# Seven products instead of eight in the first block of a gated layer's second projection, with its sums placed earlier and on two engines

## The chip, the cores and the metric

The kernel runs on one core of a Trainium2 chip. The metric is the time of one execution on the device, in microseconds (us); each figure of "the time" is a median of several runs. A profile is one further execution, taken by the hardware profiler; its engines are TensorE (PE, with its weight loads as PEld), VectorE (DVE), ScalarE (ACT), GpSimd (POOL) and SyncE (SP, which issues transfers here).

## The reference

A transformer block in float32 on x of shape (2, 1024, 256): self-attention (16 heads of 64), cross-attention to a context of shape (2, 154, 192), and a gated feed-forward layer, each with a layer norm before it and the input added after it. The part that matters here is the last:

```python
h = _layernorm(x, ln3_g, ln3_b)
p = h @ ff_w1 + ff_b1                    # (2048 tokens) x 256 x 2048
a, gate = (p[..., :D_FF], p[..., D_FF:]) # D_FF = 1024
h = a * gelu(gate) @ ff_w2 + ff_b2       # 1024 x 256
return h + x
```

## The kernel before

The first stages (self-attention, cross-attention) take the first 896 us, and nothing in them is touched. The order of instructions on each engine is the order in which the program writes them; nothing reorders it.

The gated layer takes the 2048 tokens in four **blocks** (`pair` 0 to 3) of 512 tokens, each seen as two halves j of 256. A block's first projection runs in `NF` = 8 steps (f), so there are 32 steps n. Each step has two half steps k = 2n and 2n + 1 in one loop (L1465 on): `gate_first(n)` and `gate_second(n)`. Step n's last product (`gate_last(n)`) is written inside `gate_first(n + 1)`.

The first projection is done with seven products instead of eight on a 2 x 2 partition (Strassen's method in Winograd's form): sums of weights (`weight_sums`) and sums of tokens (`token_sums`, four GpSimd instructions L1057 to L1060 a block) are made first. A step has seven 128x256 products on TensorE (L1074). VectorE takes them out of PSUM (L1103, L1105 in the first half step, L1119, L1122 in the second, L1131 in `gate_last`), ScalarE copies and makes the two gelus (L1099, L1117, L1123), and GpSimd multiplies value by gate into the layer's hidden tile `ub` (L1124 for half j = 1, L1133 for j = 0).

The second projection of a block starts when the block's hidden tile is complete, eight steps later, and is written into the half steps of the next block: the list `sums` is drained at two units a half step. It has two forms:

- `sum_slot`, the plain form, for block 0: 32 products of 128x256 (L1249), two a half step, k = 16 to 31, and four adds to x on VectorE (L1259).
- `fast_sum`, for the blocks in `FAST` (1 to 3): seven sums g of four 128x128 products each (L1219) per half j, one sum a half step, the first at k = 32. Sums 0 and 1 read hidden values as they are, sum 2 and later ones read weight sums (`quick_weights`, four 128x512 instructions L1181 to L1184) and token sums (`quick_tokens`, four 128x128 instructions a chunk c of two steps, L1196 to L1199, for each half j). Sum 0 of a half also brings an add to x on GpSimd (L1228), the others one each on VectorE (L1233).

`hold_quick` makes the tile in which the sums lie; its buffer was that of the cross-attention's transposed probabilities, last read at k = 5. `combos` is the list of sums still to be written; two a half step are taken from it. Before the change the weight sums are put there at k = 18, and block 1's token sums from k = 20 on.

Beside this, the norm of the second half of the tokens (batch entry 1) runs from k = 7 in steps at odd k, by the list `side`: a step's statistics (`stats`, two tiles, L242 and L243 on VectorE) go to the list `slow`, which `run_work` empties; one step later come the deviations (`deviation`, L248 and L252 on GpSimd), another step later the offset (L258 on VectorE) and two normalizations (L273 on GpSimd), and a step after that the transposes on TensorE (`turn`, L286). `later` holds bias adds on GpSimd (L326), one at each odd k from 17 on.

## Time and profile before

| | us |
|---|---|
| median of 3 runs | 1069.95 |
| lowest, highest | 1069.39, 1070.63 |
| the profiled execution | 1071.75 |
| its span, first to last instruction | 1069.1 |
| first product of the gated layer | 896.7 |
| block 0's second projection, first and last product | 942.0, 978.9 |
| first product of block 1's second projection | 980.8 |

A row of a timeline gives start (us from the span's start), duration, engine, line, operation, output<-inputs, shape, count, and in brackets the engine's idle time before it and what ended it. A row of the chain gives start, duration and what was done. A row of windows gives from:to, length, and for each engine its busy time and number of instructions. One fp32 matrix product is two TensorE instructions.

### The profile page before, as it was taken

The numbers are of one execution on the slowest core, as the hardware profiler recorded it, in microseconds if no ns is written. First come the engines' busy times: TensorE is split into PE (matmuls) and PEld (weight loads), VectorE is DVE, ScalarE is ACT, GpSimd is POOL, SyncE is SP. The second block draws the span as 40 slices with busy tenths as digits, with TensorE's granted clock in tenths as the row PEclk, the third lists the DMA queues.
The fourth block names the chain that finished last, engine by engine and source line by source line (L and its number), as shares of the span: only waits on it lengthen the run. The fifth ranks groups of instructions, "written<-read, shape, count | busy, mean of one in ns | idle before, by whom it ended". The sixth has DMA issues, their size and how long they took to land.

```text
span 1069.1 us, 48669 instructions
## 1 busy us (share of the span) xinstructions
PE 1057.3 (99%) x20228; PEld 709.8 (66%) x20228; DVE 882.9 (83%) x1321; ACT 645.3 (60%) x2096; POOL 774.8 (72%) x1652
## 2 busy tenths in 40 slices
PE   8999999999999999999999999999999999999998
PEld 6556756655555556657655655576866667788998
DVE  5789999998989989999999899978877887654554
ACT  5766667677666666666777676665666554342221
POOL 2677777778777777777777777676767876499984
PEclk9999999999999999999999999999999999999999
DMA  4132122021021121111102101126776545000000
GB/s 102 38 73 54 29 68 53 25 63 41 22 52 33 34 51 33 40 34 34 45 14 54 44 14 38 33 56 145 173 177 176 123 98 119 11 11 11 21 10 30
DMA packets 86046, 60.95 MB, mean 57 GB/s; under 512 B 32123, under 2 KB 74563, under 8 KB 85827
## 3 DMA queue, kind: packets, MB, share of 16 engines
q1 hardware_dynamic: 84450, 57.07, 22.0%
q8 instruction: 159, 2.61, 1.0%
q10 hardware_dynamic: 1376, 0.79, 0.2%
q14 instruction: 61, 0.49, 0.2%
HBM read 27.91 MB, written 2.10 MB: 28 GB/s over the span
## 4 chain that ended last, share of the span: by engine, by line
PE 92%; DVE 2%; DMA 2%; POOL 2%; SPq 1%; ACT 1%; issue 1%; DVEq 0%; POOLq 0%
PE po L578 20%; PE s L526 20%; PE py_ca L500 5%; PE py_sa L500 5%; PE pk_sa L369 5%; PE pq_sa L369 5%; PE pq_ca L369 5%; PE pv_sa L405 4%; PE poc L953 4%; PE pb L1074 4%; PE pq L1219 4%; PE sc L873 3%; PE pa L1074 2%; PE pc L1074 2%; PE pf L1249 1%; PE ph_ln L286 1%
## 5 line engine op out<-in xcount | busy, mean ns | idle before, releaser
L650 POOL TENSOR_SCALAR p<-p,rd,ee 128x512 f32<-128x512 f32 x512 | 390.4, 768 | 90.4 <-DVE rd L640 89.4
L537 ACT ACTIVATE p<-s,st 128x512 f32<-128x512 f32 x512 | 345.0, 686 | 175.6 <-DVE st L712 172.4
L712 DVE TENSOR_REDUCE st<-s 128x2 f32<-128x1024 f32 x256 | 308.9, 1207 | 59.6 <-issue 20.3
L675 DVE STREAM_TRANSPOSE pT<-p 128x1024 f32<-128x1024 f32 x256 | 302.8, 1220 | 2.1 <-POOL p L650 1.9
L526 PE MATMUL s<-k_sa,q_sa 64*32 64x512 f32 x4096 | 260.3, 591 | 0.8 <-DVE k_sa L390 0.6
L578 PE MATMUL po<-pT,held_v 64*32 64x256 f32 x8192 | 241.9, 376 | 0.4 <-DMA held_v<-held_v 0.4
L578 PEld LDWEIGHTS po<-pT,held_v 64*32 64x32 f32 x8192 | 177.3, 106 | 72.5 <-issue 25.2
L526 PEld LDWEIGHTS s<-k_sa,q_sa 64*32 64x32 f32 x4096 | 90.4, 106 | 91.6 <-issue 48.1
L890 ACT ACTIVATE p<-sc,neg 128x154 f32<-128x154 f32 x256 | 96.1, 404 | 76.1 <-DVE rden L898 73.3
L901 POOL TENSOR_SCALAR p<-p,rden 128x154 f32<-128x154 f32 x256 | 96.8, 399 | 49.2 <-DVE rden L898 49.0
L537 ACT ACTIVATION_READ_ACCUMULATOR p<-s,st 128x1 f32 x512 | 104.1, 203 | 0.0
L555 POOL TENSOR_TENSOR dd<-st 128x8 f32<-128x8 f32 x128 | 25.5, 199 | 71.9 <-DMA st<-st 68.5
L500 PE MATMUL py_ca<-ca_wo,o_ca 128*128 128x256 f32 x256 | 60.2, 383 | 0.0
L369 PE MATMUL pq_ca<-hT_ln,ca_wq 64*64 64x512 f32 (+1 forms) x576 | 59.4, 589 | 0.5 <-DMA ca_wq<-in_L_xattn_ca_wq_dram 0.5
L500 PE MATMUL py_sa<-sa_wo,o_sa 128*128 128x256 f32 x256 | 59.5, 386 | 0.0
L500 PEld LDWEIGHTS py_sa<-sa_wo,o_sa 128*128 128x128 f32 x256 | 47.3, 190 | 18.0 <-issue 5.0
L369 PE MATMUL pk_sa<-hT_ln,sa_wk 64*32 64x512 f32 x960 | 57.6, 590 | 0.4 <-ACT q_sa L384 0.4
L369 PE MATMUL pq_sa<-hT_ln,sa_wq 64*32 64x512 f32 (+1 forms) x976 | 57.7, 586 | 0.0
L879 DVE TENSOR_REDUCE neg<-sc 128x6 f32<-128x924 f32 (+1 forms) x48 | 47.8, 996 | 12.0 <-PE sc L873 11.8
L890 ACT ACTIVATION_READ_ACCUMULATOR p<-sc,neg 128x1 f32 x256 | 56.5, 221 | 0.0
L405 PE MATMUL pv_sa<-sa_wv,hT_ln 64*32 64x256 f32 x1792 | 53.7, 376 | 0.0
L917 DVE STREAM_TRANSPOSE pT_ca<-p 128x480 f32<-128x480 f32 (+1 forms) x96 | 52.9, 587 | 0.8 <-POOL p L901 0.8
(158 smaller groups left out, 1479.0 us busy)
## 6 DMA issues: line engine op xcount, KB each, us to landing
wf<-pT_ca SPq DMA_DIRECT2D x128, 128.0 KB, 2.4
st<-st SPq DMA_DIRECT2D x512, 1.0 KB, 1.8
held_v<-held_v SPq DMA_DIRECT2D x32, 256.0 KB, 4.1
sa_wq<-in_L_xattn_sa_wq_dram SPq DMA_DIRECT2D x32, 128.0 KB, 2.9
sa_wk<-in_L_xattn_sa_wk_dram SPq DMA_DIRECT2D x32, 128.0 KB, 3.2
sa_wv<-in_L_xattn_sa_wv_dram SPq DMA_DIRECT2D x16, 256.0 KB, 4.5
ca_wq<-in_L_xattn_ca_wq_dram SPq DMA_DIRECT2D x32, 128.0 KB, 3.8
wf<-in_L_xattn_ff_w_dram SPq DMA_DIRECT2D x12, 256.0 KB, 3.4
```

What stands on the lines that cost most here:

```text
L369: nc.tensor.matmul(pq[r][f:f + m, at:at + n], lhsT=wt[own, c, f:f + m], rhs=h[own, c, t0:t0 + n], start=(c == 0), stop=(c == NH - 1), tile ...
L405: nc.tensor.matmul(pv[r][f:f + KB, e * VC:(e + 1) * VC], lhsT=h[half, c, t0:t0 + KB], rhs=wt[half, c, :], start=(c == 0), stop=(c == NH - ...
L500: nc.tensor.matmul(py[:, e * D:(e + 1) * D], lhsT=o[:, i, (t + e) * P:(t + e + 1) * P], rhs=wo[kind][:, g * HP + i, :], start=(i == 0), st ...
L526: nc.tensor.matmul(sc[a4 * KB:(a4 + 1) * KB, j, :], lhsT=q[r, c:c + KB], rhs=k[r, h * HB:(h + 1) * HB], start=True, stop=True, tile_positi ...
L537: nc.scalar.activation(pr[:, j, :], sc[:, j, :], AF.Exp, bias=st[:, 0, 0, i, j:j + 1], accum_out=st[:, 0, 1, i, j:j + 1],)
L578: nc.tensor.matmul(po[a2][d:d + KB, :QH // 2], lhsT=v[e][r, t, d:d + KB], rhs=pT[r, d // DH * NK + n, :], start=(t == 0 and e == 0), stop= ...
L650: nc.gpsimd.tensor_scalar(pr[:, j, :], pr[:, j, :], own["rd"][:, c:c + 1], own["ee"][:, 0, c:c + 1], op0=ALU.mult, op1=ALU.mult,)
L675: nc.vector.transpose(halves[h][:, :, c:c + KB], slots[p]["p"][i].rearrange("p j (n k) -> p (j n) k", k=KB))
L712: nc.vector.tensor_reduce(st[:, 0, 0, i, :], sc[i], AX.X, ALU.max, negate=True)
L890: nc.scalar.activation(pr_[:, j, i, :T], sc[:, j, i * T:(i + 1) * T], AF.Exp, bias=neg[:, j, i:i + 1], accum_out=den[:, j, i:i + 1],)
L901: nc.gpsimd.tensor_scalar(pr_[:, j, i, :T], pr_[:, j, i, :T], rden[:, j, i:i + 1], 1.0, op0=ALU.mult, op1=ALU.mult,)
L1074: nc.tensor.matmul(into[:, :BT], lhsT=lhs, rhs=wh[pair][i], start=first, stop=True, skip_group_check=True)
```

## The change

- Block 0 takes the seven-product form too: `FAST` is now all four blocks.
- `hold_quick` and the weight sums move from k = 18 to k = 6; nothing is taken from `combos` before k = 6, and four a half step instead of two at k = 18 to 23.
- Block 0's token sums: half 0, chunks 0 and 1 go to GpSimd through `combos` (written at k = 8 to 11); half 0, chunks 2 and 3 go to VectorE through a list of their own, `in_turn`, two a half step (k = 12, 13, 16, 17); half 1, all four chunks, wait in the list `waiting` until k = 18 and then go to GpSimd (k = 18 to 21).
- In the gated layer `run_work` writes one tile's statistics a half step instead of all that stand in `slow`.

```diff
@@ run_work
-        if not spare["turned"]:
+        if slow and pools:
+            slow.pop(0)()
+        elif not spare["turned"]:
             flush(slow)
@@ gate_last
-        if pair in FAST and f % 2:
+        if pair == 0 and f % 2:
+            c = f // 2
+            (combos if c < 2 else in_turn).extend(
+                ((0, 0), fn) for fn in quick_tokens(0, 0, c, nc.gpsimd if c < 2 else nc.vector))
+            waiting.extend(((0, 1), fn) for fn in quick_tokens(0, 1, c))
+        elif pair in FAST and f % 2:
...
-    FAST = range(1, NPR)
+    FAST = range(NPR)
+    in_turn, waiting = [], []
@@ quick_tokens: the tile of the sums is looked up when a sum is written, not when it is listed
+        def s(i):
+            return quick["u", (2 * pair + j) % 4][:, (0, 1, None, 2)[i - 1], c, :]
...
-            lambda: tt(s1, a21, a22, ALU.add),
-            lambda: tt(s2, s1, a11, ALU.subtract),
+            lambda: tt(s(1), a21, a22, ALU.add),
+            lambda: tt(s(2), s(1), a11, ALU.subtract),
             lambda: tt(a21, a11, a21, ALU.subtract),
-            lambda: tt(s4, a12, s2, ALU.subtract),
+            lambda: tt(s(4), a12, s(2), ALU.subtract),
@@ the loop over half steps k
-            if k == 2 * NF + 2:
+            if k == 2 * len(CG):
                 hold_quick()
                 combos[:0] = [(None, fn) for fn in quick_weights()]
-            for _ in range(min(2, len(combos))):
+            elif k == 2 * NF + 2:
+                combos.extend(waiting)
+                waiting.clear()
+            n_mix = 0 if k < 2 * len(CG) else 4 if k in range(2 * NF + 2, 3 * NF) else 2
+            for _ in range(min(n_mix, len(combos))):
                 combos.pop(0)[1]()
+            for _ in range(min(2, len(in_turn))):
+                in_turn.pop(0)[1]()
```

(`NF` is 8 and `len(CG)` is 3, so `2 * len(CG)` is 6 and `2 * NF + 2` is 18.)

More of the change, by code (lines that the diff above doesn't have):

```diff
@@ L1187, in quick_tokens @@
     def quick_tokens(pair, j, c, engine=nc.gpsimd):
-        u, own = ub[pair][j], quick["u", (2 * pair + j) % 4]
+        u = ub[pair][j]
         (a11, a12), (a21, a22) = (
             [u[:, 2 * c + h, e * P:(e + 1) * P] for h in range(2)] for e in range(2))
-        s1, s2, s4 = (own[:, i, c, :] for i in range(3))
         tt = engine.tensor_tensor
         mixed[pair, j] = mixed.get((pair, j), 0) + 1
+        def s(i):
+            return quick["u", (2 * pair + j) % 4][:, (0, 1, None, 2)[i - 1], c, :]
         return [
-            lambda: tt(s1, a21, a22, ALU.add),
-            lambda: tt(s2, s1, a11, ALU.subtract),
+            lambda: tt(s(1), a21, a22, ALU.add),
+            lambda: tt(s(2), s(1), a11, ALU.subtract),
             lambda: tt(a21, a11, a21, ALU.subtract),
-            lambda: tt(s4, a12, s2, ALU.subtract),
+            lambda: tt(s(4), a12, s(2), ALU.subtract),
         ]
@@ L1206, in fast_sum @@
             [u[:, h::2, e * P:(e + 1) * P] for h in range(2)] for e in range(2))
-        assert g < 2 or mixed[pair, j] == NHF and (pair, j) not in [key for key, _ in combos]
+        assert g < 2 or mixed[pair, j] == NHF and (pair, j) not in [key for key, _ in combos + in_turn + waiting]
         lhs = (a11, a12, own[:, 1], a21, a22, own[:, 0], own[:, 2])[g]
```

## The prediction

> **What bounds the kernel now.** I read the page first, then the chain of waits, then engine busy time by window, then the timelines of GpSimd, VectorE and TensorE over the gated layer (894 us to the end).

> ```profile
> PE 1057.3 (99%) x20228; PEld 709.8 (66%) x20228; DVE 882.9 (83%) x1321; ACT 645.3 (60%) x2096; POOL 774.8 (72%) x1652
> ```

> TensorE is busy nearly always, so the end moves only if its work shrinks or it is made to wait. The chain gives the price of the work that is swapped:

> ```profile
> 942.14 0.86 PE pf L1249 x4
> 1053.48 12.52 PE pq L1219 x112
> ```

> A half step of the old form is two 128x256 products (four instructions), 0.86 us; block 0 has 64 such instructions, 16 x 0.86 = 13.8 us. The second row is the last block's second projection in seven products, 14 sums of 8 instructions with nothing between: 12.5 us. That is what block 0 will cost. TensorE saves 1.3 us.

> A half step k is one pass of the last loop: step n of the first projection is k = 2n and 2n+1. Block 0 is k = 0 to 15, its second projection starts at k = 16, block 1's at k = 32. The windows below run from the end of step 2's last GpSimd product (k = 6) to the end of step 15's (k = 32), and over the end of block 0.

> ```profile
> core 0: us, PE busy (x) PEld busy (x) DVE busy (x) ACT busy (x) POOL busy (x), PEclk, DMA share, GB/s
> 921.10:982.40 61.30, 60.22 (x288) 51.60 (x288) 35.46 (x92) 21.36 (x49) 52.29 (x88) 1.00 0.03 9
> 925.20:940.20 15.00, 13.92 (x65) 10.72 (x65) 12.56 (x37) 5.83 (x14) 12.55 (x22) 1.00 0.00 1
> ```

> Over these 61.3 us GpSimd works 52.3 and is free 9.0. In the second window VectorE and GpSimd both work 12.6 of 15.0 us, and this is the one place where TensorE loses time (1.1 us). The clock is 1.00. GpSimd is thus the second bound just where the change adds to it. Its rows:

> ```profile
> 920.40 0.73 POOL L1133 TENSOR_TENSOR held_v<-own 128x256 f32<-128x256 f32 x1 [5.58 <-DVE own L1131]
> 924.77 0.72 POOL L1124 TENSOR_TENSOR kT<-own 128x256 f32<-128x256 f32 x1 [3.64 <-ACT own L1123]
> 926.88 0.73 POOL L1133 TENSOR_TENSOR held_v<-own 128x256 f32<-128x256 f32 x1 [1.38 <-DVE own L1131]
> 927.56 0.72 POOL L1057 TENSOR_TENSOR hs<-hT_ln 128x256 f32<-128x256 f32 x1
> 930.42 0.72 POOL L1124 TENSOR_TENSOR kT<-own 128x256 f32<-128x256 f32 x1
> 932.17 0.73 POOL L1133 TENSOR_TENSOR held_v<-own 128x256 f32<-128x256 f32 x1
> 934.71 1.09 POOL L273 TENSOR_SCALAR xn_ln<-x,rstd_ln,off_ln 128x256 f32<-128x256 f32 x2
> 935.76 0.73 POOL L1133 TENSOR_TENSOR held_v<-own 128x256 f32<-128x256 f32 x1
> 940.56 0.72 POOL L1124 TENSOR_TENSOR kT<-own 128x256 f32<-128x256 f32 x1
> 947.84 0.73 POOL L1133 TENSOR_TENSOR u<-own 128x256 f32<-128x256 f32 x1
> 948.52 1.28 POOL L1181 TENSOR_TENSOR quick<-wf 128x512 f32<-128x512 f32 x1
> 951.10 0.73 POOL L1124 TENSOR_TENSOR u<-own 128x256 f32<-128x256 f32 x1
> 955.74 0.46 POOL L1196 TENSOR_TENSOR quick<-u 128x128 f32<-128x128 f32 x1
> 958.20 0.73 POOL L326 TENSOR_TENSOR x<-x,ff_b 128x256 f32<-128x256 f32 x1
> 979.50 0.73 POOL L1124 TENSOR_TENSOR u<-own 128x256 f32<-128x256 f32 x1 [0.64 <-ACT own L1123]
> 981.69 0.72 POOL L1133 TENSOR_TENSOR u<-own 128x256 f32<-128x256 f32 x1
> 982.38 1.00 POOL L1228 TENSOR_TENSOR x<-x,ends 128x384 f32<-128x384 f32 x1
> 983.34 0.46 POOL L1196 TENSOR_TENSOR quick<-u 128x128 f32<-128x128 f32 x1
> 1056.81 0.65 POOL L1197 TENSOR_TENSOR quick<-quick,u 128x128 f32<-128x128 f32 x1
> ```

> Prices, from start to start: a 128x256 product 0.7 (947.84 to 948.52); two weight sums 2.6 (948.52 to 951.10); the four token sums of one chunk 1.8 (955.74 to 958.20 is 2.46, less one product 0.7); the bias add of a half block 1.0 (982.38 to 983.34); block 1's four sums of the normed tokens 2.9 (927.56 to 930.42); one product with the norm's deviation pair 1.75 (930.42 to 932.17), so 1.05 for the pair; two normalizations 1.05 (934.71 to 935.76).

> ```profile
> 924.06 0.42 DVE L242 BATCH_NORM_STATS2 st_ln<-x 128x6 f32<-128x256 f32 x1
> 924.62 0.39 DVE L242 BATCH_NORM_STATS2 st_ln<-x 128x6 f32<-128x256 f32 x1
> 932.24 0.68 DVE L258 SCALAR_TENSOR_TENSOR off_ln<-mv_ln,rstd_ln 128x2 f32<-128x2 f32 x1
> 933.92 0.45 DVE L1131 SCALAR_TENSOR_TENSOR own<-pb,cols,own 128x256 f32<-128x256 f32 x1
> 934.28 0.42 DVE L1103 TENSOR_TENSOR own<-pb,own 128x256 f32<-128x256 f32 x1
> 939.08 0.48 DVE L1119 SCALAR_TENSOR_TENSOR own<-pb,cols,own 128x256 f32<-128x256 f32 x1 [0.46 <-PE pb L1074]
> 939.51 0.42 DVE L1122 TENSOR_TENSOR own<-pc,own 128x256 f32<-128x256 f32 x1
> 1054.48 0.53 DVE L1196 TENSOR_TENSOR quick<-u 128x128 f32<-128x128 f32 x1 [0.47 <-POOL u L1124]
> 1055.04 0.43 DVE L1197 TENSOR_TENSOR quick<-quick,u 128x128 f32<-128x128 f32 x1
> 1055.40 0.81 DVE L1198 TENSOR_TENSOR u<-u 128x128 f32<-128x128 f32 x1
> 1056.13 0.28 DVE L1199 TENSOR_TENSOR quick<-u,quick 128x128 f32<-128x128 f32 x1
> 1056.34 1.54 DVE L1228 TENSOR_TENSOR x<-x,ends 128x384 f32<-128x384 f32 x2
> ```
> ```profile
> 934.75 0.70 PE L1074 MATMUL pb<-hT_ln,wf 128*128 128x256 f32 x2 [0.74 <-DVE own L1103]
> 936.67 0.59 PE L1074 MATMUL pb<-hs,wf 128*128 128x256 f32 x2
> 983.03 1.05 PE L1219 MATMUL pq<-wf,u 128*128 128x128 f32 x8
> ```

> A chunk's statistics cost VectorE 0.56 (924.06 to 924.62), four token sums there 1.9 (1054.48 to 1056.34). The PE row at 934.75 is the old stall: two pairs of statistics and an offset stood ahead of L1103. The offset (L258) at 932.24 began as its deviation ended on GpSimd (932.17): no margin.

> **The change, part by part.**

> Seven products for block 0: minus 1.3 us of TensorE, as above. VectorE gets 12 adds for 4, after k = 16. Outside the second window it works 35.5 - 12.6 = 22.9 us of 46.3, half the time, so I cost that at nothing; if that cover were gone, it would be eight adds of at most 0.42 (L1122's row, twice their size), 3.4 us.

> Weight sums: 5.2 us of GpSimd, moved from k = 18 and 19 to k = 6 and 7. Their cover is the idle time before 924.77; the first two fit there (921.1 to 923.7), the last two, queued behind the product at 924.77, run 925.5 to 928.0 and push everything behind them, step 3's product first, 1.2 us late.

> Token sums: 32 instructions, 24 on GpSimd. Eight stand at k = 8 to 11 (3.6 us), sixteen at k = 18 to 21 (7.1). Two bias adds, at k = 16 and 23, bring 2.0. So GpSimd gets 12.7 us more between k = 6 and k = 32, the weight sums aside.

> Where that ends: block 1's second sum (983.03) reads the product that GpSimd started at 981.69 and ended at 982.4, a margin of 0.6. From here GpSimd's lateness is TensorE's. With all 9.0 us of idle filled, the excess is 12.7 - 9.0 - 0.6 = 3.1 us; 1.1 of the idle cannot be filled (923.7 to 924.8 comes before the product it waits for), so 4.2. What TensorE saved ahead of this point is contained in it.

> The waits add to that. GpSimd's queue after the change: step 3's product ends at 928.7, the four normed-token sums 931.6, two token sums 932.5, step 4's first product 933.2, two more 934.1, deviation about 935.0 (before: 932.2). VectorE stands at that offset from 932.2 to 935.0 with step 5's evacuations queued behind it: offset to 935.7 (0.68), one statistic 936.3, L1131 and L1103 (0.36, 0.42) 937.1, and only then the product that started at 934.75. TensorE is 2.4 us late.

> GpSimd goes on: product 935.7, two token sums 936.6, product and two sums 938.1, deviation 939.1, normalizations 940.2, step 5's last product 940.9 (before: 936.5). Here the new wait bites. VectorE's first two token sums, at k = 12, read that product, so VectorE stands until 940.9; then two sums (0.95), a statistic, and L1119 (0.43) to 942.8. Step 6's next TensorE product needs that L1119: 942.85 where it was 936.67, 6.2 late. And GpSimd waits in turn: L1122, the gelu and its product take 1.05 from L1122's start (939.51 to 940.56), so it idles from 940.9 to 943.8. Product, deviation, normalizations, product: 947.3. The same loop leaves it idle some 0.7 before step 7's first product and 1.3 before step 8's (estimates by the same steps; VectorE's sums at k = 16 again wait for step 7's last product). So 948.0 + 0.7 + 1.05 + 1.05 + 0.7 = 951.5, the bias add 952.5, idle to 953.8, and 0.7 + 1.05 + 0.7 + 0.7 (product, normalizations, a 0.7 bias row, product): what ended at 948.5 (947.84, k = 18) ends at 956.9.

> From there to step 15's product GpSimd took 33.8 us (948.6 to 982.4), 0.64 of it idle (979.50). It loses the weight sums (5.2) and gets 7.1 + 1.0: 33.8 - 0.6 - 5.2 + 8.1 = 36.1. So 956.9 + 36.1 = 993.0, and block 1's second sum starts there, not at 983.03: 10.0 later. TensorE, 6 to 7 us late by its own waits and 1.3 ahead by its sums, could be there by 989, so GpSimd sets it. Behind it GpSimd has 3.2 us a step (two products, four token sums) against TensorE's 4.8 (seven products of 0.43, two sums of 12.52/14), and all goes as before.

> Spread statistics: they take away most of the old stall (up to the window's 1.1 us), but the offsets' wait takes its place. Nothing is gained as long as GpSimd is late.

> [...]

> Sum: +10.0 us. The profiled execution took 1071.75 us (span 1069.1 and 2.65 around it); it would take 1081.75. The median of the runs is 1069.95, so 1080.0.

> **The rivals.**

> *Packing only, 1074.* The VectorE waits cost GpSimd no further idle time, and 4.2 us are left. For it: the 9.0 us of idle. Against: each wait is in a queue in order. Chance 0.21.

> *The cover holds, faster: 1067.5.* GpSimd's early sums vanish in its idle time before 927, the spread statistics end TensorE's 1.1 us of stall and the 1.3 come too: minus 2.4. It decides if GpSimd's excess at k = 33 stays under the 0.6 margin. Against: 12.7 us against 9.0. Chance 0.07.

> *Both by halves, within 0.2%.* The excess is some 2 us, as if a token sum were cheaper than its row. 0.2% of the time (2.1 us) is about what a measurement of this kernel tells from no change. Chance 0.06.

> *The engines hinder each other, 1083.* The GpSimd row at 1056.81 took 0.65 rather than 0.46 while VectorE added two operands (1056.34): 0.2 us for each overlap, and eight token sums and their loop make some 3 us. [...] Chance 0.10.

> **How the numbers follow.** The forecast has 0.56. Slower are 0.56 + 0.21 + 0.10 = 0.87, same 0.06, faster 0.07. The range goes from below the packing case, 1073, to above the last, 1084; about 0.17 is left out (0.13 below, the rest above).

> **What would show it.** Right: the first two weight sums before step 3's product, GpSimd near 9 tenths from 925 to 993, TensorE idle some 8 us between 930 and 953 behind VectorE's evacuations and 2 to 4 us near block 1's first sums behind GpSimd, VectorE's token sums waiting for the GpSimd product, seven-product sums at 0.89 a half step in block 0. Wrong: step 15's product ending before 984, or TensorE without idle time at k = 8 to 16.

## The result, and the profile after

| | before | after the change |
|---|---|---|
| median, us | 1069.95 (5 runs, 1068.08 to 1070.63) | 1079.58 (5 runs, 1078.89 to 1081.25) |
| the profiled execution | 1071.75 | 1081.25 |
| its span | 1069.1 | 1079.5 |
| start of step 2's last GpSimd product (k = 6) | 920.40 | 919.29 |
| from there to the end | 148.7 | 160.2 |

The change made the kernel slower: ratio 1.0096, interval 1.0085 to 1.0107. From k = 6 to the end it takes 11.5 us longer (160.2 - 148.7). What lies ahead of that is untouched by the new sums, and in the profiles below it ends anywhere between 919.3 and 922.2 us. So the stretch from there to the end, and not the span, is what I compare between profiles; it is called the gated part. In the changed kernel the numbers of the later lines are two to eleven higher (in its variants by a few more): L1103 is L1105, L1119 is L1121, L1131 is L1133, L1133 is L1135, the token sums are L1207 to L1210, the second projection's matmul is L1230.

The page of the changed kernel, busy times, granted clock by slice, and shares of the chain:

```profile
PE 1061.9 (98%) x20276; PEld 710.7 (66%) x20276; DVE 886.9 (82%) x1337; ACT 646.9 (60%) x2098; POOL 790.5 (73%) x1678
...
PEclk9999999999999999999999999999999999899999
...
PE 83%; POOL 7%; DMA 3%; DVE 2%; SPq 2%; ACT 1%; issue 1%; POOLq 0%; ACTq 0%; DVEq 0%
```

TensorE has less to do and is yet busy 4.6 us longer (1061.9 against 1057.3), and one slice shows a lower clock (8 tenths where the others have 9): some of its work ran slowly. GpSimd holds 7% of the chain, where it held 2%: the chain now runs through it from the weight sums at 924.38 to the product that ends at 993.5, with few breaks, the longest of them TensorE's from 941.53 to 946.85.

Busy time by window, the changed kernel (columns: PE, PEld, DVE, ACT, POOL, then the granted TensorE clock):

```profile
921.10:982.40 61.30, 55.87 (x298) 48.02 (x297) 35.50 (x98) 19.37 (x45) 52.34 (x92) 0.92 0.02 7
...
925.00:993.00 68.00, 60.67 (x321) 52.06 (x319) 37.37 (x104) 21.15 (x50) 59.91 (x109) 0.91 0.03 9
930.00:953.00 23.00, 17.91 (x74) 13.53 (x72) 11.34 (x34) 5.91 (x14) 17.17 (x32) 0.78 0.00 1
...
936.00:946.00 10.00, 8.39 (x21) 5.63 (x22) 4.80 (x17) 2.17 (x5) 7.13 (x14) 0.51 0.01 2
```

In the 61.3 us that the prediction counted, GpSimd is free 9.0 us, as before, though it has 12.7 us more to do: the work did not fill the gaps, it moved the end. Step 15's product comes 73.5 us behind the start of the gated part (992.82 less 919.29) where it came 61.3 behind it (981.69 less 920.40), 12.2 later. From 936 to 946 TensorE's granted clock is 0.51. Before, it was 1.00 in the whole stretch. There is a second, shorter fall of the clock near block 1's first sums, behind TensorE's wait there:

```profile
987.48:990.89 3.41, 1.52 (x10) 1.25 (x9) 0.20 (x1) 0.42 (x2) 3.33 (x8) 1.00 0.00 0
990.89:994.31 3.42, 3.19 (x13) 2.63 (x12) 0.91 (x2) 0.83 (x2) 3.42 (x6) 0.50 0.01 2
```

The waits of TensorE from 915 to 1000 (engine, line, whom it waited for: total, times, longest), and the timelines of the three engines, all of the changed kernel:

```profile
PE pb L1076 <- DVE own L1105: 3.4, 1, 3.4
PE pq L1230 <- POOL u L1135: 2.1, 2, 1.9
PE ph_ln L286 <- POOL xn_ln L273: 1.0, 1, 1.0
PE pb L1076 <- DVE own L1121: 0.9, 2, 0.5
```
```profile
923.66 0.73 POOL L1126 TENSOR_TENSOR kT<-own 128x256 f32<-128x256 f32 x1 [1.06 <-ACT own L1125]
...
933.20 0.71 POOL L252 TENSOR_TENSOR rstd_ln<-var_ln,power 128x2 f32<-128x2 f32 x1
...
939.17 0.73 POOL L1135 TENSOR_TENSOR held_v<-own 128x256 f32<-128x256 f32 x1
942.43 0.73 POOL L1126 TENSOR_TENSOR kT<-own 128x256 f32<-128x256 f32 x1 [2.53 <-ACT own L1125]
...
947.91 0.73 POOL L1126 TENSOR_TENSOR kT<-own 128x256 f32<-128x256 f32 x1 [1.94 <-ACT own L1125]
...
951.42 1.00 POOL L1239 TENSOR_TENSOR x<-x,ends 128x384 f32<-128x384 f32 x1
954.24 0.73 POOL L1126 TENSOR_TENSOR u<-own 128x256 f32<-128x256 f32 x1 [1.82 <-ACT own L1125]
...
956.70 0.73 POOL L1135 TENSOR_TENSOR u<-own 128x256 f32<-128x256 f32 x1
...
992.82 0.72 POOL L1135 TENSOR_TENSOR u<-own 128x256 f32<-128x256 f32 x1
```
```profile
933.95 0.67 DVE L258 SCALAR_TENSOR_TENSOR off_ln<-mv_ln,rstd_ln 128x2 f32<-128x2 f32 x1 [3.14 <-POOL rstd_ln L252]
...
939.94 0.29 DVE L1207 TENSOR_TENSOR quick<-held_v 128x128 f32<-128x128 f32 x1 [3.73 <-POOL held_v L1135]
940.26 0.29 DVE L1208 TENSOR_TENSOR quick<-quick,held_v 128x128 f32<-128x128 f32 x1
...
951.50 1.07 DVE L1207 TENSOR_TENSOR quick<-held_v 128x128 f32<-128x128 f32 x1 [2.04 <-POOL held_v L1135]
```
```profile
935.92 0.91 PE L1076 MATMUL pb<-hT_ln,wf 128*128 128x256 f32 x2 [3.42 <-DVE own L1105]
...
941.53 1.22 PE L1076 MATMUL pb<-hs,wf 128*128 128x256 f32 x2 [0.51 <-DVE own L1121]
942.55 1.06 PE L1076 MATMUL pb<-hs,w1s 128*128 128x256 f32 x2
943.40 1.06 PE L1076 MATMUL pc<-hs,w1s 128*128 128x256 f32 x2
...
993.60 0.79 PE L1230 MATMUL pq<-wf,u 128*128 128x128 f32 x2 [0.23 <-POOL u L1135]
```

They tell one story. VectorE stands 3.14 us at the offset, because GpSimd's deviation (933.20) is behind the weight sums and four token sums; L1105 is queued behind that, and TensorE waits 3.42 us for it. VectorE stands again, 3.73 us, at its first token sum until GpSimd's product of 939.17 is done; L1121 follows, TensorE goes on at 941.53, and now GpSimd has to wait for what TensorE starts so late: 2.53, 1.94 and 1.82 us. From 956.70 GpSimd is packed (it works nearly without a pause), and block 1's sum at 993.60 waits for its product. The products at 942.55 and 943.40 stand 0.85 us apart, where two of before stood 0.43 apart (941.12 and 941.55): that is the clock, 0.50 in those us where it was 1.00 before.

### The profile page after: what moved, and what is told of

It is laid out like the page before. It is cut to its first block, busy times and chain, and to the rows that moved or that the text cites. A ratio compares the mean times of both kernels' runs of the same rounds, so it can differ in the third digit from the quotient of the medians.

```text
span 1079.5 us, 48811 instructions
## 1 busy us (share of the span) xinstructions
PE 1061.9 (98%) x20276; PEld 710.7 (66%) x20276; DVE 886.9 (82%) x1337; ACT 646.9 (60%) x2098; POOL 790.5 (73%) x1678
## 4 chain that ended last, share of the span: by engine, by line
PE 83%; POOL 7%; DMA 3%; DVE 2%; SPq 2%; ACT 1%; issue 1%; POOLq 0%; ACTq 0%; DVEq 0%
PE po L578 18%; PE s L526 18%; PE py_ca L500 5%; PE py_sa L500 5%; PE pq_ca L369 4%; PE pq_sa L369 4%; PE pv_sa L405 4%; PE pk_sa L369 4%; PE poc L955 4%; PE pq L1230 3%; PE sc L875 3%; PE pb L1076 3%; DMA st<-st 2%; SPq L547 2%; PE pa L1076 2%; PE pc L1076 2%
## 5 line engine op out<-in xcount | busy, mean ns | idle before, releaser
L578 PEld LDWEIGHTS po<-pT,held_v 64*32 64x32 f32 x8192 | 177.0, 106 | 73.5 <-issue 27.6
L881 DVE TENSOR_REDUCE neg<-sc 128x6 f32<-128x924 f32 (+1 forms) x48 | 47.8, 997 | 12.6 <-PE sc L875 12.4
```

The costliest lines, as they stand in the source:

```text
L578: nc.tensor.matmul(po[a2][d:d + KB, :QH // 2], lhsT=v[e][r, t, d:d + KB], rhs=pT[r, d // DH * NK + n, :], start=(t == 0 and e == 0), stop= ...
```

## The experiments

The theory: the loss is GpSimd's queue ahead of block 1's first sums, made longer by VectorE standing in order behind it (offset, token sums). The first rival: the amount of the work alone, wherever it is done. The clock came in after the first profile. The kernel before was measured again with each group of runs; a ratio is to its median there, which was 1070.95 us for the first three runs below and for kept_warm.

**VectorE's eight token sums to GpSimd** (pool_tokens), which takes away the second wait and makes GpSimd's load larger:

```diff
-            (combos if c < 2 else in_turn).extend(
-                ((0, 0), fn) for fn in quick_tokens(0, 0, c, nc.gpsimd if c < 2 else nc.vector))
+            combos.extend(((0, 0), fn) for fn in quick_tokens(0, 0, c))
```

> The changed kernel, but half 0's chunks 2 and 3 are summed on GpSimd as well (eight sums, 3.6 us more work there) and none on VectorE. Theory (VectorE standing in its queue for GpSimd is what widens the loss): VectorE no longer stands for 3.7 us at k = 12 and 2.0 us at k = 16, so GpSimd does not idle 2.5 and 1.9 us before the products of steps 6 and 7; those 4.4 + 1.8 us go, 3.6 come. Step 15's last product is some 2.9 us earlier and the time falls to 1076.7 (1075 to 1078), though GpSimd does more. Rival (GpSimd's amount of work alone sets the time): 3.6 us slower, 1083.

Measured: 1079.49 us, ratio 1.0084 (1.0069 to 1.0099); gated part 157.7, so 2.5 less than the change (1.7 less than its repeat below) with eight more instructions on GpSimd. That is less than was forecast, and the interval overlaps the change's; the rival's 1083 is excluded. TensorE's waits and GpSimd's row ahead of step 7's first product:

```profile
PE pb L1076 <- DVE own L1105: 3.4, 1, 3.4
PE pq L1229 <- POOL u L1135: 2.4, 1, 2.4
...
```
```profile
946.98 0.73 POOL L1126 TENSOR_TENSOR kT<-own 128x256 f32<-128x256 f32 x1 [0.62 <-ACT own L1125]
```

The wait behind L1121 is gone and GpSimd's idle time there falls from 1.94 to 0.62. The amount of work alone would have made it slower. The offset's wait, 3.4, stays, as it should.

**Half 1's sixteen token sums left out** (half1_out); that half's products read plain tiles:

```diff
-            waiting.extend(((0, 1), fn) for fn in quick_tokens(0, 1, c))
...
+        if (pair, j) == (0, 1):
+            lhs = (a11, a12, a11, a21, a22, a12, a21)[g]
```

> The changed kernel, but the sixteen token sums of block 0's half 1 (k = 18 to 21) are left out, and its sums 2 to 6 read hidden values that were not summed. Theory (GpSimd's lateness at k = 33 is paid by TensorE a second time): GpSimd reaches step 15's product 7.1 us earlier, at about 986.4, before TensorE asks for it; the stalls at block 1's first two sums and the slow products behind them go, 4.1 us, 1075.5 (1074.5 to 1076.5). Rival (only the first stall, before 946 us, costs): no change, 1079.6.

Measured: 1077.84, ratio 1.0066 (1.0051 to 1.0081), above the forecast range, though the kernel before was itself 1.0 us slower here than in the result; gated part 155.4, 4.8 less (4.0 less than the repeat). TensorE's waits no longer name GpSimd's `u`:

```profile
PE pb L1076 <- DVE own L1105: 3.4, 1, 3.4
PE pb L1076 <- DVE own L1121: 0.9, 2, 0.5
PE ph_ln L286 <- POOL xn_ln L273: 0.7, 1, 0.7
```

So GpSimd's load from k = 18 on is on the path to the end, as its packing says, and 6.7 of the 11.5 us are there without it.

**All 32 left out** (no_tokens; the products of block 0 read plain tiles):

```diff
-            (combos if c < 2 else in_turn).extend(
-                ((0, 0), fn) for fn in quick_tokens(0, 0, c, nc.gpsimd if c < 2 else nc.vector))
-            waiting.extend(((0, 1), fn) for fn in quick_tokens(0, 1, c))
+            pass
...
+        if pair == 0:
+            lhs = (a11, a12, a11, a21, a22, a12, a21)[g]
```

> The changed kernel, but all 32 token sums of block 0 are left out, and its sums 2 to 6 read hidden values that were not summed; the early weight sums, the spread statistics, seven products and the two bias adds stay. Theory (the whole loss comes from where the token sums are done): what stays are 1.3 us saved and at most 1.2 us of GpSimd's weight sums running into k = 8: 1069.3 (1068.0 to 1070.5). Rival (the early weight sums or the spreading cost as much): 1072 or more.

Measured: 1069.64, ratio 0.9988 (0.9978 to 0.9998), as the theory had it; gated part 149.5, 0.8 above before. The token sums are thus 10.7 of the 11.5 us by the profiles and all of the loss by the ratios (0.9988 against 1.0096). The profiled execution is one of the slower ones: the mean granted clock was 1.000 in eight of the ten executions, which took 1067.9 to 1070.4 us, and 0.998 in the two that took 1071.9 and 1072.4, the profiled one among them. Without the token sums the seven products do save time, 0.2 to 2.4 us by the interval.

**The weight sums alone moved** (weights_early: before with the weight sums at k = 6):

```diff
-            if k == 2 * NF + 2:
+            if k == 2 * len(CG):
```

> The kernel before with one edit of the change: the weight sums at k = 6 and 7. Theory: their last 1.2 us push GpSimd's queue, VectorE stands for the offset at k = 11 that much longer ahead of two statistics, TensorE stalls some 2 us at k = 13 and may be granted half its clock for one stretch: 1.2 to 2.8 us slower, ratio 1.0011 to 1.0026. Rival (they vanish in GpSimd's idle time, which was the cover that the edit counts on): 1.0000.

Measured: 1072.85 against 1071.65, ratio 1.0008 (0.9999 to 1.0017), under the forecast range and not clear of no change; gated part 149.7, 1.0 more. The old stall grows from 0.74 to 1.77 us, the product's row being

```profile
937.55 0.70 PE L1074 MATMUL pb<-hT_ln,wf 128*128 128x256 f32 x2 [1.77 <-DVE own L1103]
```

**The statistics alone spread** (spread_alone: before with the edit in `run_work`):

```diff
-        if not spare["turned"]:
+        if slow and pools:
+            slow.pop(0)()
+        elif not spare["turned"]:
```

> The kernel before with one edit of the change: one tile's statistics a half step. Theory: the old stall at VectorE's statistics shrinks by some 0.5 us, but the transposes at k = 15 wait for GpSimd's normalizations, whose queue is as long as before, and take it back: 0 to 0.5 us faster, ratio 0.9995 to 1.0000 to the kernel before. Rival (the stall of 1.1 us was VectorE's alone): 1.1 us faster, 0.9990.

Measured: 1070.27 against 1071.65, ratio 0.9993 (0.9985 to 1.0002); the stall is 0.6 where it was 0.74. Nothing that can be told from no change.

**Full clock by extra work** (kept_warm: the change with 30 transposes of the identity put on TensorE ahead of the second half of step 6, for nothing but to keep it busy):

```diff
+            if k == 2 * NF - 3:
+                warm = sum_tile("warm")
+                for _ in range(30):
+                    nc.tensor.transpose(warm[:, :P], ident, ident)
```

> The changed kernel with 30 transposes of the identity put into TensorE's queue ahead of the second half of step 6 (k = 13), where TensorE stands 3.4 us; they fill the wait and nothing reads them. What is asked: between 936 and 946 us products follow each other at 0.85 us rather than 0.43, and the granted clock was 0.84 to 0.90 there. If TensorE's idle time brings the low clock, the products behind stay at 0.43, GpSimd gets its inputs sooner, and the time falls by 1 to 2 us, to 1078. If the clock comes from something else, no change or 0 to 1 us slower.

Measured: 1082.08, ratio 1.0105 (1.009 to 1.012): a miss. Windows:

```profile
937.00:941.00 4.00, 1.98 (x10) 1.06 (x9) 0.66 (x3) 0.47 (x1) 3.84 (x9) 1.00 0.00 0
943.00:948.00 5.00, 5.00 (x12) 4.01 (x13) 3.40 (x12) 2.16 (x5) 3.38 (x6) 0.50 0.00 0
```

The clock was kept at the first wait and fell after the next ones (1.66, 0.21 and 1.29 us, from 938 to 943). The time came out where the other branch of the expectation had it, but not for its reason. One place was not enough, so the clock's price was still open.

**Full clock at every wait** (all_warm: transposes at four places):

```diff
+        if n == NF - 1:
+            keep_warm(10)
...
+            if k == 2 * NF - 3:
+                keep_warm(30)
...
+            if k == 2 * NF - 3:
+                keep_warm(14)
...
+            if k == 4 * NF:
+                keep_warm(20)
```

> The changed kernel with transposes of the identity in each of TensorE's waits: 30 ahead of the second half of step 6, 14 behind it, 10 inside step 7's first half, 20 ahead of block 1's first sum; nothing reads them. What is asked: what the half clock behind these waits costs. If it delays GpSimd's inputs by 1.2 and 0.5 us, as the idle times before the products of steps 7 and 8 exceeded the prediction's, and stretches the products between block 1's first sums: 1 to 2.5 us less than the change, ratio 1.0073 to 1.0087 to the kernel before. Rival (the clock costs nothing, since GpSimd sets the end): 1.0096. Its profile should show the clock at 1.00 all through.

Measured: 1079.6 against 1071.65, ratio 1.0072 (1.006 to 1.0084); gated part 157.7. The window of the half clock now reads

```profile
936.00:946.00 10.00, 9.07 (x51) 6.49 (x49) 6.14 (x22) 2.65 (x7) 7.16 (x14) 1.00 0.00 0
```

The clock is worth 2.5 us of the gated part against the change and 1.7 against its repeat, 2.6 to 4.1 by the ratios (1.0096 and, below, 1.0110 against 1.0072), whose intervals reach 1.2 to 1.7 us to each side. Between 7.7 (ratio) and 9.0 us (gated part) of loss remain at full clock. GpSimd's first products of steps 7 and 8 show what the clock had cost there, and what it had not:

```profile
946.70 0.73 POOL L1134 TENSOR_TENSOR kT<-own 128x256 f32<-128x256 f32 x1
953.01 0.73 POOL L1134 TENSOR_TENSOR u<-own 128x256 f32<-128x256 f32 x1 [1.82 <-ACT own L1133]
```

Ahead of step 7's product GpSimd no longer idles, where it idled 1.94; ahead of step 8's it idles 1.82 as in the change.

**The change once more** (change_again), to see whether the clock falls each time:

> The change as it is, in the same session as the last kernel and with a profile of its own. The lowered clock was seen in one profile of the change and in those of its variants. If it belongs to the kernel: ratio 1.0085 to 1.0107 again, the clock at half for about 10 us from 936 to 946 us. If it was that execution's: the time as TensorE's full clock would give it, 1.007.

Measured: 1083.21 against 1071.35, ratio 1.0110 (1.0095 to 1.0126); gated part 159.4, the clock from 936 to 946 at 0.52, the wait for L1105 again 3.4. The second fall, near 991 us, is missing in this profile.

**All token sums on VectorE, later** (later_vector: k = 17 to 26, three weight sums early and the fourth at k = 18, the two products that need no token sum put first):

```diff
+            in_turn.extend(((0, 0), fn) for fn in quick_tokens(0, 0, c, nc.vector))
+            waiting.extend(((0, 1), fn) for fn in quick_tokens(0, 1, c, nc.vector))
...
+                order = [(0, 0), (0, 1), (1, 0), (1, 1), None, None] + order[2:7] + order[9:]
```

> Seven products in all blocks, placed by what the profiles show: three weight sums at k = 6 and 7 (they fit ahead of step 3's product), the fourth at k = 18; all 32 token sums of block 0 on VectorE at k = 17 to 26, where it is half idle; block 0's sums 0 and 1 of both halves first (k = 16 to 19), two half steps without a sum, then sums 2 to 6. Spread statistics stay. Theory (the loss was the place of the sums): no stall beyond that of before, TensorE's 1.3 us saved: 1.3 us faster (0.5 to 2), ratio 0.9988 (0.9980 to 0.9995). Rival (VectorE's two-input adds hold up GpSimd, which works nearly without a pause there, or are held up by it): GpSimd reaches step 15's product late, 1 to 4 us slower, 1.001 to 1.004.

Measured: 1072.84 against 1071.65, ratio 1.0016 (1.0008 to 1.0024): a miss, and the rival's side in the time. VectorE, then GpSimd, the same stretch, and the product of TensorE behind them:

```profile
946.85 0.81 DVE L1209 TENSOR_TENSOR quick<-held_v 128x128 f32<-128x128 f32 x1
947.70 0.70 DVE L1210 TENSOR_TENSOR quick<-quick,held_v 128x128 f32<-128x128 f32 x1
949.42 1.22 DVE L1211 TENSOR_TENSOR held_v<-held_v 128x128 f32<-128x128 f32 x1
...
955.29 0.28 DVE L1211 TENSOR_TENSOR held_v<-held_v 128x128 f32<-128x128 f32 x1
```
```profile
946.76 0.75 POOL L326 TENSOR_TENSOR x<-x,ff_b 128x256 f32<-128x256 f32 x1
947.48 0.77 POOL L1135 TENSOR_TENSOR u<-own 128x256 f32<-128x256 f32 x1
...
949.22 1.26 POOL L1194 TENSOR_TENSOR quick<-wf,quick 128x512 f32<-128x512 f32 x1
```
```profile
952.89 0.70 PE L1076 MATMUL pb<-hT_ln,wf 128*128 128x256 f32 x2 [1.12 <-DVE own L1105]
```

An add takes 0.28 us where GpSimd rests (955.29). Where a GpSimd instruction of 0.75, 0.77 or 1.26 us began first in these rows, the add ended 0.15 to 0.16 us after that one: 947.66 after 947.51, 948.40 after 948.25, 950.64 after 950.48. That looks like waiting and not like running slowly. TensorE then waits for evacuations queued behind such adds, up to 1.12 us; for GpSimd at block 1's first sums it does not wait here.

**Token sums divided** (split_tokens: both halves' chunks 0 and 1 on GpSimd, 2 and 3 on VectorE, from k = 17, up to two a half step on each engine; three weight sums early, and the other moves named in the expectation):

```diff
+            for j in range(2):
+                own = quick_tokens(0, j, c, nc.gpsimd if c < 2 else nc.vector)
+                shares[c // 2, j].extend(((0, j), fn) for fn in own)
...
+            if k > 2 * NF:
+                for i in range(2):
+                    turns = shares[i, 0] or (shares[i, 1] if k > 2 * NF + 5 else [])
+                    for _ in range(min(2, len(turns))):
+                        turns.pop(0)[1]()
```

> Seven products in all blocks, the work shared as the profiles suggest: three weight sums at k = 6 and 7, the fourth at k = 22; of each half's token sums, chunks 0 and 1 on GpSimd and chunks 2 and 3 on VectorE (k = 17 to 20 and 22 to 25, two a half step on each); sums 0 and 1 of both halves first; the first sum's add to x on VectorE; the bias adds that block 1 needs later put behind k = 32; block 1's sums start one half step later. Theory (place, not amount, is what lost the time, and each engine's free time in k = 17 to 31 takes half of the token sums): 1.3 us saved, less 0.5 to 1 of short stalls on VectorE: ratio 0.9990 (0.9982 to 1.0005). Rival (the two engines hold each other up whenever both add two operands): 1 to 3 us slower, 1.001 to 1.003.

Measured: 1073.47 against 1071.35, ratio 1.0021 (1.0011 to 1.003): a miss. TensorE waits for half 1's last token sums (L1214) and for the fourth weight sum (L1198) on GpSimd:

```profile
PE pq L1236 <- POOL quick L1214: 2.4, 1, 2.4
PE pq L1236 <- POOL quick L1198: 0.8, 1, 0.8
```

**Divided with less on GpSimd** (split_less: three of eight chunks on GpSimd, none of the token sums before k = 17, block 0's bias adds on VectorE, the additions of L326 kept out of k = 22 to 32):

```diff
+                first = c < 2 - j
+                own = quick_tokens(0, j, c, nc.gpsimd if first else nc.vector)
...
-                (nc.vector if pair == NPR - 1 else nc.gpsimd).tensor_tensor(
+                (nc.vector if pair in (0, NPR - 1) else nc.gpsimd).tensor_tensor(
```

> The kernel with the split token sums, mended where its profile shows TensorE waiting for GpSimd (0.8 us for the fourth weight sum, 2.4 us for half 1's token sums): the fourth weight sum at k = 18, half 1's chunk 1 on VectorE too (12 of its 16 sums there, three a half step), half 1's sums 2 to 6 one half step later. Theory (these two waits were all that was lost against the 1.3 us saved): ratio 0.9990 (0.9982 to 1.0002), no wait of TensorE over 1.2 us behind k = 16. Rival (the work moved to VectorE meets GpSimd's there, as where all 32 sums stood on VectorE, and stalls TensorE by some 1 to 2 us): 1.0000 to 1.0015.

Measured: 1070.1 against 1071.23, ratio 0.9992 (0.9981 to 1.0003); gated part 148.5. The same 32 sums and seven products cost nothing that shows in this order:

```profile
PE pb L1076 <- DVE own L1105: 0.6, 1, 0.6
PE pb L1076 <- DVE own L1121: 0.5, 1, 0.5
...
```

That the seven products' 1.3 us come out as a gain is not shown here: the interval holds both 1.0 us of gain and none. Several things were moved at once (also the bias adds and the adds of L326), and which of them it needed was not taken apart.

## Why the prediction was right, and where not

**The path.** The forecast's mechanism held step by step. The profile after began its gated part 1.1 us earlier than before, so the times of its ledger (the list of what GpSimd and VectorE do one after the other) are read less 1.1. GpSimd's product of step 5 was to end at 940.9, thus 939.8; it ended at 939.90. L1119 (now L1121) was to be done at 942.8; TensorE's product behind it was due at 942.85, thus 941.75, and began at 941.53. From the product at k = 18 to block 1's second sum the ledger had 36.1 us; from 957.43 to 993.60 it was 36.2. TensorE was there early (its wait of 1.9 us stands at 989.77) and GpSimd set the time.

**What undoing showed.** The weight sums' 1.2 us in the queue measured 1.0 in the profile (weights_early; the ratio alone does not show it). The two VectorE waits are real and separate: pool_tokens takes one away and leaves the other. The spread statistics gained nothing. The work itself does not force the loss: split_less has it all.

**The step that was mis-sized.** The prediction has no term for a lower TensorE clock, and two of its idle times came out longer. GpSimd's idle time (us) ahead of the first products of steps 6, 7 and 8:

| | step 6 | step 7 | step 8 |
|---|---|---|---|
| the ledger | 2.9 | 0.7 | 1.3 |
| the change | 2.53 | 1.94 | 1.82 |
| its repeat | 2.53 | 1.58 | 1.82 |
| all_warm, at full clock | 2.52 | none | 1.82 |

Step 7's excess is the clock, 0.51 from 936 to 946: at full clock GpSimd does not idle there at all, so the ledger's 0.7 was itself too much. Step 8's excess is not the clock, since all_warm has it too: in both, VectorE's first token sum took 1.07 us there, beside GpSimd's bias add, and in the change the pair at 951.50 was through at 952.90, in 1.40 where the ledger had 0.95. Step 6's was shorter because the pair at 939.94 and 940.26, which met no GpSimd instruction, was through at 940.55, in 0.61 rather than 0.95.

So the product at k = 18 came at 957.43 where the ledger, less 1.1, had 955.8, 1.6 late, and the gated part is +11.5 (the change) and +10.7 (the repeat) for +10.0; at full clock it is +9.0, and the ledger 1 us too high. Some 0.5 of that lies behind block 1's second sum: six of its eight instructions had run before the wait (from 991.88; 993.60 is the last two), so that from there to the end it is 85.5 us in all_warm and in the repeat, 85.9 in the change, where the ledger kept the 86.1 of before (1069.1 less 983.03). The errors went against each other, and that the median came within 0.5 us of the forecast is luck to that extent; so is that the profile's start and what lies outside its span (1.75 us for 2.65) offset the rest.

**The signs.** TensorE's idle time from 930 to 953 was to be some 8 us; it was 5.1 (23.0 less 17.91), and the half clock made up for it. GpSimd was to be busy near 9 tenths from 925 to 993: 59.91 of 68.0. Behind GpSimd 2 to 4 us near block 1's sums: 2.1. The first two weight sums ran ahead of step 3's first product (923.66), the other two right behind it. VectorE's token sums waited for GpSimd's products (3.73 and 2.04). Step 15's product ended at 993.5, not before 984.

**The rivals.** Packing only falls with pool_tokens and the second wait of 3.73 us. That the engines hinder each other happens, but not for 3 us here: the add at 951.50 took 1.07 us and ended 0.15 after GpSimd's of 951.42; the other seven met no GpSimd instruction. By these rows the hindrance is most of step 8's excess, about 0.5 us; in later_vector TensorE's waits of 1.12 and 0.77 us stand behind such adds.

## What to carry over

An instruction given to a half idle engine is priced by the queues: what stands behind it there, and who stands in order behind a wait for that (VectorE stood 3.14 and 3.73 us here). Write the ledger of both queues to the next point where an engine off the path meets the one on it; an idle share of 9 us absorbed next to nothing here (12.7 us of work put GpSimd 12.2 later), because the idle time was itself a wait for the late chain. The same work, divided by what must be early and what may be late, cost nothing that shows.

## What the runs showed of the hardware

```profile
933.85:937.26 3.41, 1.61 (x8) 1.06 (x9) 3.34 (x11) 0.65 (x2) 3.25 (x7) 1.00 0.03 5
```
```profile
932.87:936.28 3.41, 0.35 (x2) 0.30 (x2) 2.22 (x6) 0.14 (x1) 3.19 (x7) 1.00 0.00 0
936.28:939.69 3.41, 2.31 (x7) 1.23 (x6) 0.00 (x0) 0.00 (x0) 3.25 (x7) 0.50 0.02 5
939.69:943.10 3.41, 2.90 (x9) 1.91 (x8) 3.06 (x12) 1.26 (x4) 0.88 (x2) 0.50 0.00 0
943.10:946.52 3.42, 3.42 (x10) 2.70 (x9) 1.85 (x6) 0.91 (x2) 2.72 (x6) 0.50 0.00 0
```

By these rows TensorE was busy 1.61 of 3.41 us, under half, ahead of the fall in no_tokens. In the change the clock stayed at 0.50 behind the stretches that were busy 2.31 and 2.90 and was 1.00 again behind the full one; at the second fall (shown with the result) it was 1.00 again behind one of 3.19. In the seven profiles with falls the stretches measured ahead of them were busy 0.35 to 1.61 us. In weights_early the wait of 1.77 us leaves each stretch around it at least 1.64 us of work, more or less by where it begins (five windows of 3.41 us that begin 0.5 us apart, from 934.00 to 936.00, are busy 1.64 to 1.86), and the clock stayed at 1.00. What decides between 1.61 and 1.64, and whether the busy time alone does, these runs do not show. One kernel can fall in one execution and not in another: no_tokens did in two of ten, by the mean clock (0.998 against 1.000).

Short waits close together can thus cost more than their sum: in no_tokens 1.64 and 0.21 us of waiting were followed by 3.42 us at half clock.

**VectorE's two-operand adds ended with GpSimd's instructions** where the two met: in later_vector 0.28 us alone and up to 1.22 beside an instruction of 1.26, the three shown with that run ending 0.15 to 0.16 us after GpSimd's. In split_less such adds took 0.82 and 1.35 us (948.09 and 948.83) and 0.28 (951.03), and TensorE never waits more than 0.6: there the long adds did not set the time. The rows of before that the prediction shows (1054.48 to 1056.34) give a mean price of 0.47, 1.9 us for four against 1.8 on GpSimd; that held only with both at work: in the change four sums that met no one took 1.1 us in all (939.94 to 940.55 and 941.73 to 942.20).
